# A decoder layer with a two-expert feed-forward part: places a half step later, gates' weights in steps, one sequence of expert tiles, deeper result and place buffers

## The chip, the core and the metric

One core of a Trainium2 chip runs the whole program. Its engines are TensorE (PE, with weight loads shown apart as PEld), VectorE (DVE), ScalarE (ACT), GpSimd (POOL) and SyncE (SP), which issues most of the DMAs. Each engine takes its instructions in the order in which they were written. The metric is the device time of one execution in microseconds (us); the time before is 1168.72 us, the median of three runs.

## What is computed

The reference is one pre-norm decoder layer on x of 64 sequences x 128 tokens x 128 features, in float32:

```
x = x + self_attention(layernorm(x))            # 16 heads of 8
x = x + cross_attention(layernorm(x), ctx)      # 77 context tokens, mask
x = x + ffn(layernorm(x))

ffn:  proj = x @ Wp.T;  scores = l2norm(proj) @ l2norm(sim).T / temperature     # 8 experts
      the two highest scores, softmax over the two -> weights
      out = sum over the two experts of weight * (gelu(x @ W1[e] + b1[e]) @ W2[e] + b2[e])
```

## The kernel before

**Attention.** A unit is one sequence (block); four blocks make a group (GB = 4), so there are 16 groups of self-attention jobs and then 16 of cross-attention. One loop (line 863) runs over all 128 blocks, each in two **half steps**; eight half steps are one group. A half step writes, in this order: PE's scores (`score_tiles`, L707, and the mask's bias, L716), DVE's maxima (L726) and ACT's exponentials (L753); then one entry of `soon`; statistics; then, in every second half step, a norm from `bits` and the values (L768), in the others entries of `todo` (the next group's transposes, query, key and value products, the output product) and a norm from `bits`; then **at most one entry of `late`, in the list's order, if its due half step has come**; then one scatter from `sending`; then, in three of eight half steps, one DMA of weights or constants. Scores use three PSUM banks (`ps_s`), of which a half step takes two; small products share two banks (`ps_m`, tag mm).

**The prologue of the next group** (line 608) is four norms through `bits`, then its products through `todo`. With its fourth norm it writes two POOL instructions: `add_row` (L233) and, for cross-attention, the mask's bias (L624).

**Routing.** After a cross group's output is added, `route(g)` (line 300) puts seven steps into `late`, due LATER = (6, 7, 8, 10, 11, 12, 13) half steps on: `trans` (L240), `project(0)` and `project(1)` (products with the gates' weights, L325; ACT's squares, L331; after the second, POOL's chain from ssq, L335, to rnorm, L212), `largest(0)` and `largest(1)` (DVE; the first begins with L345, which reads rnorm), `count` (POOL sums `ahead`, L381) and `place` (PE multiplies `both`, L391, and `ahead`, L394; DVE makes the places). Then eight scatters (L428, POOL, indirect DMA), one per half step, write the group's normalised rows to their places in `part.x` in DRAM, sorted by expert. Since a group takes eight half steps, the steps of one group lie between those of the next.

**Two parts.** Groups 0 to 10 are part 0 and groups 11 to 15 part 1, each with its own `part.x` and `part.y` in DRAM. `table(part)` finds which 256 rows and which expert each tile has. Unused rows are filled by DMAs from SP: `spare` (L274, 7 per part, written one per slot after the expert weights) and `tail_zeros` (L480). Scatters and tail zeros of a part are declared free of dependences among themselves (`apart`), and fetches wait for all that is in `part.scatters`; the spares are in neither.

**Gates' weights.** `finish_weights` (L106 to L111) and `gate_weights` (L286 to L298) prepare the cross-attention's biases and the product of the projection with the normalised expert vectors. They run once, through `todo`.

**Experts.** `experts(part)` (line 949) goes over the part's tiles (51 and 27). For tile t it writes `turn(t+1)` (transposes, L974; copy, L976; places `at`, L978), `hidden(t)` (L989, then ACT, L996), `output(t-1)` (L1007, DVE's addition L1013, and two scatters by POOL, L1018, to `part.y`) and `fetch(t+3)` (SP loads 256 rows, L961; DVE copies the expert's weights, L968). Results `yr` have three buffers, places `at` four; each is free when its scatters have landed or been read. Part 0's tiles begin beside the last half steps of the attention; later tiles are each followed by one entry of what is left of the lists (`rest`) and one scatter. Then part 1's tiles run as a second sequence, each followed by one or two gathers of part 0's results (L1048, SP) and their weighted sums (`combine`, L1054, DVE). At the end come the 20 gathers of part 1. All groups' rows stay in SBUF (`xs`) and leave as they are finished (L1059).

Of the kernel before, what the change touches and what calls it, by code (L numbers as in the profile page):

```python
# [15 lines left out]
P = 128  # L16
# [9 lines left out]
LATER = (6, 7, 8, 10, 11, 12, 13)  # L26
NORM = 2
SPLIT = 11
# [3 lines left out]
def decoder_layer(  # L32
# [71 lines left out]
    def finish_weights():  # L104

        nc.vector.tensor_scalar(W["bq_s"], W["bq_s"], float(DH) ** -0.5, None, ALU.mult)  # L106
        t = work.tile([P, P], F32, tag="bvb", name="bvb", bufs=1)
        nc.vector.tensor_copy(t, W["bv_s"].to_broadcast([P, P]))
        pb = ps_m.tile([P, D], F32, tag="mm", name="pb")
        nc.tensor.matmul(pb, t, W["co_s"], start=True, stop=True)  # L110
        nc.vector.tensor_tensor(W["bo_s"], pb, W["bo_s"], ALU.add)  # L111
# [145 lines left out]
    class Part:  # L257
# [14 lines left out]
        def spare(self, n):  # L272
            at = E * self.step + n * TILE
            nc.sync.dma_start(  # L274
                self.x[at : at + TILE, :].rearrange("(p h) d -> p h d", p=P), zero
            )

# [3 lines left out]
    def gate_weights():  # L281
# [9 lines left out]
        nc.gpsimd.tensor_scalar(sq, W["sim_s"], rn, None, ALU.mult)  # L291
        pt = ps_m.tile([P, E], F32, tag="mm", name="pt")
        nc.tensor.transpose(pt, sq, ident[:E, :E])
        snT = work.tile([P, E], F32, tag="snT", name="snT", bufs=1)
        nc.vector.tensor_copy(snT, pt)
        pg = ps_m.tile([P, E], F32, tag="mm", name="pg")
        nc.tensor.matmul(pg, W["wp_s"], snT, start=True, stop=True)
        nc.vector.tensor_copy(wpg[:, D:], pg)  # L298

    def route(g):  # L300
# [62 lines left out]
        def count():  # L363
# [23 lines left out]
            )  # L387

# [132 lines left out]
    newest, sending, clearing, gathered = [None], [], [], []  # L521
# [14 lines left out]
    def attention(beside):  # L536
# [293 lines left out]
        late, soon, now, bits, pieces, coming = [], [], [0], [], [], []  # L830
# [30 lines left out]
        steps, todo = [], []  # L861

        for s in range(NB + LAG + 3):
# [11 lines left out]
            if s == 13 * GB:  # L875
                todo.append(finish_weights)
                todo.append(gate_weights)
# [4 lines left out]
            for half in range(2):  # L882
# [10 lines left out]
                if soon:  # L893
                    soon.pop(0)()
                if half == s % 2 and n < NGRP:
# [41 lines left out]
        def rest():  # L937

            for queue in (soon, todo, bits, late, pieces):
                if queue:  # L940
                    f = queue.pop(0)
                    (f[1] if queue is bits or queue is late else f)()
# [6 lines left out]
    def experts(part, ff, ps_h, ps_y):  # L949
        flat = we_s.rearrange("p e w -> p (e w)")  # L950
        N = part.tiles
        V = [dict() for _ in range(N)]

        def fetch(t):
            v = V[t]
            v["x"] = ff.tile([P, 2, DX], F32, tag="x", name="xr", bufs=4)
# [13 lines left out]
        def turn(t):  # L970
# [6 lines left out]
            v["at"] = ff.tile([P, 2], I32, tag="at", name="at", bufs=4)  # L977
# [24 lines left out]
        def output(t):  # L1002
            v = V[t]
            py = ps_y.tile([P, 2, D], F32, tag="y", name="py")
# [7 lines left out]
            y = ff.tile([P, 2, D], F32, tag="y", name="yr")  # L1012
# [162 lines left out]
```

## Time and profile before

| | |
|---|---|
| runs | 1168.72, 1167.09, 1172.84 us |
| the profiled execution | 1172.9 us, span of its instructions 1171.2 us |
| PE busy | 1071.0 us (91%) |
| DVE, ACT, POOL busy | 748.3 (64%), 612.6 (52%), 603.7 us (52%) |
| mean granted PE clock | 0.948 |
| self-attention, about | 24 to 400 us |
| cross-attention, about | 400 to 819 us |
| expert tiles, PE | 817 to 1145.3 us |
| last gathers, sums and stores | 1145 to 1171 us |

How to read it: the page cuts the span into 40 equal slices; each digit is an engine's busy share in tenths, and PEclk is the clock that PE was granted. A list of waits gives the waiting line, what ended the wait, the total, the number of times and the longest. A timeline gives start, length, engine, line, operation and tiles (out<-in), and in brackets the idle time before with what ended it; a wait for several things is put down to the last of them that the profile shows, which need not be the true one. The letter q marks an engine's queue (an issue, not work). A table of stages gives each engine's busy time, the number of its instructions and the granted clock.

### The profile page before, as it was taken

Reading aid. Unit: us, or ns where it says so; the run is one execution under the profiler, and the core shown is the slowest. Engines: PE = TensorE matmul, PEld = TensorE weight load, DVE = VectorE, ACT = ScalarE, POOL = GpSimd, SP = SyncE. Lnnn points to the kernel's source line nnn. Section 1 sums busy time; section 2 is a strip of 40 time slices with the busy share of each in tenths; the row PEclk is TensorE's granted clock in tenths of the full one; section 3 lists DMA queues with packets and bytes.
Section 4 is the critical chain, followed back from the end, with each engine's and each line's share of the span. In section 5 each row is a group of like instructions: output and inputs, shape, how many; then the busy total and the mean of one; then the engine's idle time right before and its main releaser. Section 6 shows DMA issues by size and latency. Waiting matters only on the chain.

```text
span 1171.2 us, 39936 instructions
## 1 busy us (share of the span) xinstructions
PE 1071.0 (91%) x15925; PEld 874.9 (75%) x15925; DVE 748.3 (64%) x2139; ACT 612.6 (52%) x1378; POOL 603.7 (52%) x1313
## 2 busy tenths in 40 slices
PE   5999999999899999998889899999989899979990
PEld 3777777777677777776666677777888899969990
DVE  3588778788767656665656666776545454446655
ACT  3266556566556556664555556655545444424440
POOL 8122232232321323666565667667788886646661
PEclk9699999899989999998999989999989899989996
DMA  4233342333333322332222212221222242125544
GB/s 116 54 68 61 68 70 61 68 79 73 67 87 88 88 70 70 86 89 67 71 81 69 75 53 76 63 66 50 60 73 68 63 122 76 55 85 149 151 117 143
DMA packets 95561, 93.55 MB, mean 80 GB/s; under 512 B 23615, under 2 KB 77908, under 8 KB 95376
## 3 DMA queue, kind: packets, MB, share of 16 engines
q1 hardware_dynamic: 73280, 57.58, 22.1%
q0 software_dynamic: 9088, 16.94, 4.6%
q10 hardware_dynamic: 13008, 16.49, 4.5%
q8 instruction: 125, 2.05, 0.8%
q14 instruction: 60, 0.49, 0.2%
HBM read 49.69 MB, written 43.09 MB: 79 GB/s over the span
## 4 chain that ended last, share of the span: by engine, by line
PE 59%; DMA 13%; POOL 11%; issue 6%; DVE 6%; ACT 2%; SPq 2%; DVEq 0%; POOLq 0%; ACTq 0%
PE ps L707 12%; PE pt L707 9%; PE po L768 8%; PE py L1007 6%; PE ph L989 6%; POOL yr L1018 5%; DMA qh<-md 4%; PE pt L716 4%; PE ps L716 3%; DMA d<-kT 3%; PE pq L651 2%; POOL xr L428 2%; PE py L807 2%; PE pk L663 2%; PE tp L240 1%
## 5 line engine op out<-in xcount | busy, mean ns | idle before, releaser
L726 DVE TENSOR_REDUCE m<-ps 128x4 f32<-128x512 f32 (+1 forms) x512 | 275.0, 577 | 185.8 <-PE ps L716 105.4
L753 ACT ACTIVATE e<-pt 128x512 f32<-128x512 f32 (+1 forms) x512 | 277.0, 590 | 220.8 <-PE pt L716 113.8
L707 PE MATMUL pt<-qh,kh 32*128 32x128 f32 (+1 forms) x4096 | 325.2, 286 | 12.6 <-DMA qh<-md 10.8
L707 PE MATMUL ps<-kh,qh 31*128 31x128 f32 (+1 forms) x4096 | 327.6, 293 | 6.7 <-DVE m L726 4.7
L707 PEld LDWEIGHTS ps<-kh,qh 31*128 31x128 f32 x4096 | 276.6, 195 | 73.5 <-issue 31.7
L707 PEld LDWEIGHTS pt<-qh,kh 32*128 32x128 f32 (+1 forms) x4096 | 265.3, 169 | 18.8 <-issue 8.4
L996 ACT ACTIVATE hT<-ph,wr 128x256 f32<-128x256 f32 x312 | 128.6, 471 | 161.0 <-issue 127.7
L1018 POOL DMA_INDIRECT yr<-yr,at x156 | 165.9, 1064 | 87.0 <-DVE yr L1013 63.6
L428 POOL DMA_INDIRECT xr<-x,slot x128 | 133.2, 1041 | 73.8 <-ACT e L753 34.0
L217 POOL TENSOR_SCALAR var<-stat 128x4 f32<-128x4 f32 x48 | 11.1, 231 | 291.2 <-DVE stat L203 290.9
L1007 PEld LDWEIGHTS py<-wr,hT 128*128 128x128 f32 x1248 | 153.8, 194 | 8.9 <-DVE yr L1013 3.4
L1007 PE MATMUL py<-wr,hT 128*128 128x128 f32 x1248 | 154.6, 278 | 4.2 <-DVE yr L1013 4.2
L989 PE MATMUL ph<-xT,wr 128*128 128x256 f32 x624 | 152.1, 388 | 2.3 <-DVE at L978 1.8
L768 PE MATMUL po<-e,vm 128*32 128x128 f32 (+1 forms) x4096 | 145.2, 285 | 0.0
L768 PEld LDWEIGHTS po<-e,vm 128*32 128x32 f32 (+1 forms) x4096 | 108.8, 113 | 31.8 <-issue 24.3
L989 PEld LDWEIGHTS ph<-xT,wr 128*128 128x128 f32 x624 | 115.4, 195 | 16.3 <-issue 2.4
L716 PE MATMUL pt<-ident_b,bias 128*77 128x512 bf16 x256 | 96.0, 393 | 0.0
L1013 DVE TENSOR_TENSOR yr<-py,wr 128x256 f32<-128x256 f32 x78 | 33.1, 424 | 90.4 <-PE py L1007 90.1
L968 DVE COPY wr<-we_s 128x1157 f32 x78 | 61.6, 789 | 35.1 <-DVE yr L1013 32.5
L716 PE MATMUL ps<-bias,ident_b 128*128 128x308 bf16 x256 | 78.1, 310 | 0.0
L227 ACT ACTIVATE xn<-xs,shift,rstd 128x128 f32<-128x128 f32 x128 | 62.1, 491 | 28.0 <-POOL shift L221 8.1
L202 DVE BATCH_NORM_STATS2 st<-xs 128x6 f32<-128x128 f32 x192 | 54.4, 283 | 6.3 <-DMA xs<-in_x_dram 4.1
(173 smaller groups left out, 1351.4 us busy)
## 6 DMA issues: line engine op xcount, KB each, us to landing
xr<-xr SPq DMA_DIRECT2D x78, 130.0 KB
d<-qT ACTq DMA_DIRECT2D x32, 256.0 KB
qh<-d SPq DMA_DIRECT2D x128, 64.0 KB
r<-yr SPq DMA_DIRECT2D x64, 128.0 KB
d<-kT ACTq DMA_DIRECT2D x16, 256.0 KB
kh<-d SPq DMA_DIRECT2D x64, 64.0 KB
out_dram<-xs SPq DMA_DIRECT2D x16, 256.0 KB
xr<-zero SPq DMA_DIRECT2D x30, 130.0 KB
```

What stands on the lines that cost most here:

```text
L227: nc.scalar.activation(v["xn"][:, b, 0:D], xs[g][:, b, :], AF.Identity, bias=shift[:, i : i + 1], scale=rstd[:, i : i + 1],)
L428: i = nc.gpsimd.indirect_dma_start(out=part.x, out_offset=bass.IndirectOffsetOnAxis(ap=slot[:, g * GB + b, k : k + 1], axis=0), in_=v["xn" ...
L707: nc.tensor.matmul(pt[:, r, :], v[still][rows, r, b, :], v[moving][rows, r, b, :], start="bias" not in v or r == 0, stop="bias" not in v,)
L716: nc.tensor.matmul(pt, left, right.unsqueeze(1).to_broadcast([P, HG, K]), start=False, stop=True,)
L726: nc.vector.tensor_reduce(v["m", b // 2][:, c, :, b % 2], v.pop(("ps", b, c)), AX.X, ALU.max, negate=True,)
L753: i = nc.scalar.activation(e[:K], pt[:K], AF.Exp)
L768: nc.tensor.matmul(v["o"][32 * c : 32 * c + 32, b % 2, :, j // 2, :], w[:, at : at + 32], v["e", b, c][:K, j, :].rearrange("p (n q) -> p n ...
L968: nc.vector.tensor_copy(v["w"], flat[:, bass.ds(w, WE)])
L989: nc.tensor.matmul(ph[:, c % 2, :], v["w"][:, c * P : (c + 1) * P], v["xT"], start=True, stop=True,)
L996: i = nc.scalar.activation(v["h"][:, n, :], ph[:, n % 2, :], AF.Gelu, bias=v["w"][:, WF + n : WF + n + 1],)
L1007: nc.tensor.matmul(py[:, h, :], v["h"][:, c, h * P : (h + 1) * P], v["w"][:, F + c * D : F + (c + 1) * D], start=(c == 0), stop=(c == NFC ...
L1018: i = nc.gpsimd.indirect_dma_start(out=part.y, out_offset=bass.IndirectOffsetOnAxis(ap=v["at"][:, h : h + 1], axis=0), in_=y[:, h, :], in_ ...
```

## The change

- LATER's last entry goes from 13 to 14 (`place`), and after `count` the list `rest` skips two tiles.
- `finish_weights` and `gate_weights` become generators, of which one piece is written per half step, from block 52 on, instead of all in one half step.
- The spare rows' DMAs join the group `apart` and the list `part.scatters`.
- `experts` runs once over the tiles of both parts (78). `rest` and the scatters go on until 48 tiles have been output; the gathers of part 0 start once the first tile of part 1 has been output.
- Results `yr` have six buffers instead of three, places `at` eight instead of four.

```diff
--- before.py
+++ after.py
@@ -23,8 +23,9 @@
 NEG = -(2.0 ** 100)
 LAG = 4
 TILE = 256
-LATER = (6, 7, 8, 10, 11, 12, 13)
+LATER = (6, 7, 8, 10, 11, 12, 14)
 NORM = 2
+AHEAD = 3
 SPLIT = 11
 
 
@@ -106,8 +107,10 @@
         nc.vector.tensor_scalar(W["bq_s"], W["bq_s"], float(DH) ** -0.5, None, ALU.mult)
         t = work.tile([P, P], F32, tag="bvb", name="bvb", bufs=1)
         nc.vector.tensor_copy(t, W["bv_s"].to_broadcast([P, P]))
+        yield
         pb = ps_m.tile([P, D], F32, tag="mm", name="pb")
         nc.tensor.matmul(pb, t, W["co_s"], start=True, stop=True)
+        yield
         nc.vector.tensor_tensor(W["bo_s"], pb, W["bo_s"], ALU.add)
 
 
@@ -271,9 +274,11 @@
 
         def spare(self, n):
             at = E * self.step + n * TILE
-            nc.sync.dma_start(
+            i = nc.sync.dma_start(
                 self.x[at : at + TILE, :].rearrange("(p h) d -> p h d", p=P), zero
             )
+            apart(i.ins, f"x{self.n}")
+            self.scatters.append(i.ins)
 
     parts = [Part(0, 0, SPLIT), Part(1, SPLIT, NGRP)]
 
@@ -289,12 +294,17 @@
         nc.vector.reciprocal(sn, W["tmp_s"])
         nc.gpsimd.tensor_tensor(rn, rn, sn, ALU.mult)
         nc.gpsimd.tensor_scalar(sq, W["sim_s"], rn, None, ALU.mult)
+        yield
+        yield
         pt = ps_m.tile([P, E], F32, tag="mm", name="pt")
         nc.tensor.transpose(pt, sq, ident[:E, :E])
         snT = work.tile([P, E], F32, tag="snT", name="snT", bufs=1)
+        yield
         nc.vector.tensor_copy(snT, pt)
+        yield
         pg = ps_m.tile([P, E], F32, tag="mm", name="pg")
         nc.tensor.matmul(pg, W["wp_s"], snT, start=True, stop=True)
+        yield
         nc.vector.tensor_copy(wpg[:, D:], pg)
 
     def route(g):
@@ -385,6 +395,7 @@
             nc.gpsimd.tensor_tensor(
                 part.seen, ahead[:, GB - 1, :], both[:, GB - 1, :], ALU.add
             )
+            return "apart"
 
         def place():
             pr = ps_m.tile([P, GB * E], F32, tag="mm", name="pr")
@@ -518,7 +529,7 @@
             needs, sums, tails, experts_past, expert, tiles_past, first, places,
         ]
 
-    newest, sending, clearing, gathered = [None], [], [], []
+    newest, sending, clearing, gathered, ready = [None], [], [], [], [0]
 
     def apart(inst, group):
 
@@ -827,7 +838,7 @@
 
             soon.append(other)
 
-        late, soon, now, bits, pieces, coming = [], [], [0], [], [], []
+        late, soon, now, bits, pieces, coming, idle = [], [], [0], [], [], [], []
 
         def prepare(n):
 
@@ -858,7 +869,7 @@
         constants()
         clean(2)
         background = load_experts()
-        steps, todo = [], []
+        steps, todo, weights = [], [], []
 
         for s in range(NB + LAG + 3):
             if s == NB + 1:
@@ -873,8 +884,7 @@
                 if s // GB + 2 < len(jobs):
                     steps = prepare(s // GB + 2)
             if s == 13 * GB:
-                todo.append(finish_weights)
-                todo.append(gate_weights)
+                weights.extend((finish_weights(), gate_weights()))
             if s % GB == 3:
                 todo += steps
                 steps = []
@@ -892,6 +902,8 @@
                 arrived = len(coming)
                 if soon:
                     soon.pop(0)()
+                if weights and next(weights[0], weights) is weights:
+                    weights.pop(0)
                 if half == s % 2 and n < NGRP:
                     stats(s + 12)
                     if b == GB - 1:
@@ -936,23 +948,29 @@
 
         def rest():
 
+            if idle:
+                idle.pop()
+                return True
             for queue in (soon, todo, bits, late, pieces):
                 if queue:
                     f = queue.pop(0)
-                    (f[1] if queue is bits or queue is late else f)()
+                    if (f[1] if queue is bits or queue is late else f)() == "apart":
+                        idle.extend((None, None))
                     return True
             return False
 
         return rest
 
 
-    def experts(part, ff, ps_h, ps_y):
+    def experts(ff, ps_h, ps_y):
         flat = we_s.rearrange("p e w -> p (e w)")
-        N = part.tiles
+        order = [(part, t) for part in parts for t in range(part.tiles)]
+        N = len(order)
         V = [dict() for _ in range(N)]
 
         def fetch(t):
             v = V[t]
+            part, t = order[t]
             v["x"] = ff.tile([P, 2, DX], F32, tag="x", name="xr", bufs=4)
             v["w"] = ff.tile([P, WE], F32, tag="w", name="wr", bufs=4)
             row = nc.sync.value_load(
@@ -974,7 +992,7 @@
                 nc.tensor.transpose(tp[:, h * P : (h + 1) * P], v["x"][:, h, 0:D], ident)
             v["xT"] = ff.tile([P, TILE], F32, tag="xT", name="xT")
             nc.vector.tensor_copy(v["xT"], tp)
-            v["at"] = ff.tile([P, 2], I32, tag="at", name="at", bufs=4)
+            v["at"] = ff.tile([P, 2], I32, tag="at", name="at", bufs=8)
             nc.vector.scalar_tensor_tensor(
                 v["at"], v["x"][:, :, D], v["w"][:, WE - 1 :], v["x"][:, :, D + 1],
                 ALU.is_lt, ALU.add,
@@ -1001,6 +1019,7 @@
 
         def output(t):
             v = V[t]
+            part, _ = order[t]
             py = ps_y.tile([P, 2, D], F32, tag="y", name="py")
             for h in range(2):
                 for c in range(NFC):
@@ -1009,7 +1028,7 @@
                         v["w"][:, F + c * D : F + (c + 1) * D],
                         start=(c == 0), stop=(c == NFC - 1),
                     )
-            y = ff.tile([P, 2, D], F32, tag="y", name="yr")
+            y = ff.tile([P, 2, D], F32, tag="y", name="yr", bufs=6)
             nc.vector.tensor_tensor(
                 y, py, v["w"][:, WB : WB + D].unsqueeze(1).to_broadcast([P, 2, D]), ALU.add
             )
@@ -1024,7 +1043,6 @@
                 apart(i.ins, f"y{part.n}")
             v.clear()
 
-        AHEAD = 3
         for t in range(min(AHEAD, N)):
             fetch(t)
             yield
@@ -1037,6 +1055,7 @@
                 hidden(t)
             if t > 0:
                 output(t - 1)
+                ready[0] = t
             if t + AHEAD < N:
                 fetch(t + AHEAD)
             yield
@@ -1084,25 +1103,27 @@
                     pools.append(ctx.enter_context(tc.tile_pool(
                         name=name, bufs=bufs, space=bass.MemoryType.PSUM, reuse_waits="tile"
                     )))
-                first.append(experts(parts[0], *pools))
+                first.append(experts(*pools))
             if n < 4 or n > 4:
                 next(first[0])
 
         rest = attention(beside)
-        for _ in first[0]:
-            rest()
-            if sending:
-                sending.pop(0)([newest[0]])
-            if clearing:
-                clearing.pop(0)()
-        assert not rest() and not sending and not clearing
         ff = pools[0]
-
 
         done = [(g, b) for g in range(SPLIT) for b in range(GB)]
         total, steps = len(done), parts[1].tiles
-        for t, _ in enumerate(experts(parts[1], *pools)):
-            for _ in range(len(done) - total + min(total, (t + 1) * total // steps)):
+        for _ in first[0]:
+            t = ready[0] - parts[0].tiles
+            if t <= -AHEAD:
+                rest()
+                if sending:
+                    sending.pop(0)([newest[0]])
+                if clearing:
+                    clearing.pop(0)()
+            if t == -AHEAD:
+
+                assert not rest() and not sending and not clearing
+            for _ in range(len(done) - total + max(0, min(total, t * total // steps))):
                 if len(gathered) > 3:
                     combine()
                 gather(parts[0], ff, *done.pop(0))
```

## The prediction

> **What bounds the kernel now.** I read the slices of the page first, then what TensorE (PE) waited for, then the timelines around each wait.
>
> ```profile
> PE   5999999999899999998889899999989899979990
> PEclk9699999899989999998999989999989899989996
> ```
>
> PE is busy in nearly every slice, so time can only be won where it stands still or where its clock drops, and both digits dip in the same slices. The list of PE's waits names the places:
>
> ```profile
> PE pr L394 <- POOL ahead L381: 19.4, 9, 3.8
> ...
> PE tp L974 <- DMA xr<-xr: 8.6, 3, 7.8
> ...
> PE py L1007 <- DVE yr L1013: 4.2, 3, 3.0
> PE pt L293 <- POOL bvb L291: 3.5, 1, 3.5
> PE pb L110 <- DVE bvb L108: 2.3, 1, 2.3
> ```
>
> (total us, times, longest.) A wait costs more than its length. After the one at 545 us and the one at 318 us the stage table shows a granted clock (column PEclk) of 0.50:
>
> ```profile
> 318.70:328.90 10.20, 6.45 (x87) 5.34 (x90) 2.42 (x7) 1.87 (x5) 3.82 (x11) 0.50 0.37 89
> 547.40:554.20 6.80, 6.80 (x75) 4.82 (x74) 1.92 (x6) 2.67 (x5) 3.20 (x11) 0.50 0.32 62
> ...
> 239.00:246.00 7.00, 5.62 (x121) 4.14 (x124) 5.21 (x16) 3.73 (x8) 2.50 (x8) 1.00 0.23 41
> ```
>
> The third row follows an idle of 1.38 us (before 240.68) and keeps 1.00; an idle of 1.70 us (before 153.33) was followed by a half clock. So I price each wait by the length of its stage, not by the wait. The stages: in PE's timeline the first L707 product of every half step gives its start; eight half steps are one group.
>
> **Part A: spare rows out of the dependence chain.** Groups of the cross phase that start at 456.57, 481.67 and 507.45 last 25.10, 25.79 and 25.79 us. The next five (533.24 to 691.34) last 31.95, 30.19, 30.72, 31.69 and 33.55: 158.10 against 5 x 25.79 = 128.95, **29.15 us** too much. In just these the 14 spare-row DMAs (L274) are issued, 540.6 to 666.5:
>
> ```profile
> 540.63 0.36 SPq L274 DMA_DIRECT2D xr<-zero  x1
> ...
> 543.41 0.96 POOL L428 DMA_INDIRECT xr<-x,slot  x1 [4.05 <-ACT qT L654]
> 544.66 0.76 POOL L381 TENSOR_TENSOR ahead<-ahead,both 128x8 f32<-128x8 f32 x3
> ...
> 545.48 0.41 PE L394 MATMUL pr<-ahead,ones_f 128*128 128x32 f32 x2 [2.87 <-POOL ahead L381]
> ```
>
> ACT is named but was long done; the scatter starts 2.8 us after the spare DMA into the same tensor, about the 2.3 to 5.0 us a scatter takes to land. POOL waits for it, `ahead` is queued behind, and PE behind that. The diff puts the spares into the scatters' group, so neither waits for the other; fetches wait for them instead, over 130 us later, when they have long landed; SP issues the same 14 DMAs in the same places. Even if some wait stayed, the longest of these five PE waits (3.2) is about the half step (3.1 to 3.5) by which place moves. Gain 29.15; two shorter waits at 776.8 and 800.4 (0.61, 0.46) go too: **30.2**.
>
> The Trainium skill, "TensorE: Matmul & The Clock Gate", section "What's actually happening", says the clock halves after an idle window of about 3.4 us; by that none of these five waits (2.6 to 3.2 us) would halve it and A would give the 14.3 us of waits alone. The rows above disagree, so the sum goes by stage length.
>
> **Part B: place at 14 collides with trans.** A new group enters `late` every 8 half steps, its trans due at 6: the same half step as the previous group's 14. The eight scatters follow their place, one per half step, and still fill just eight. But the list pops one entry per half step, in order, so trans, project 0 and project 1 each slip one half step; largest 0 (due at 10) does not. The half step now free for project 1 is the one in which the next group's fourth norm issues add_row and bias on POOL, ahead of it. Today, in that half step (starts 501.85, the next 504.58):
>
> ```profile
> 506.65 0.20 POOL L212 TENSOR_TENSOR rnorm<-rnorm,newton 128x4 f32<-128x4 f32 x1
> ...
> 507.12 0.15 DVE L345 TENSOR_TENSOR gate<-raw,rnorm 128x32 f32<-128x32 f32 x1
> ...
> 507.52 2.00 DVE L357 TENSOR_TENSOR h<-gate,v 128x32 f32<-128x32 f32 x1
> ...
> 508.19 1.27 POOL L233 TENSOR_TENSOR xs<-xs,bo_s 128x512 f32<-128x512 f32 x1
> ```
>
> rnorm is ready at 506.85 and DVE needs it at 507.12: 0.27 us to spare. Afterwards POOL does, from the end of the fourth norm (505.66): L233 1.27, L624 1.27, small gaps, to 508.4, then the chain from ssq to rnorm, 2.70 (504.15 to 506.85): ready at 511.1. DVE is there at 507.12 + 0.66 (project's four matmuls, now in this half step) = 507.8 and **waits 3.3 us**; queued behind it are the maxima that free the score banks, and PE waits for those. In return L357 loses its 2.00 us: where no L233 runs beside it (769 us on) it takes 0.19. So largest 0 ends at 511.15 + 1.32 (its length at 815.41) = 512.5 instead of 510.5 (end of L361), 2.0 later; PE is itself 0.66 later there, having got that time back earlier in the group, so about **1.5 us** of new idle per group (the 0.2 us that PE waited there in 11 groups counted). 1.5 lies between the idles that kept (1.38) and lost (1.70) the clock; the group with the latter was 2.74 longer than its neighbours (22.94 against 20.20). I take 2.0. Bounds: -0.3 (the wait hidden, place's nine DVE instructions moved to an emptier half step) and 4.5 (3.3 in full, plus 1.2 of half clock). It happens in the 10 groups that still have a prologue to come: **+20**, bounds -3 and +45. The last three routed groups have no add_row but also lose their spare half step: +1.
>
> The Trainium skill, "SBUF — State Buffer", section "Who interferes with whom", says a DVE instruction with two SBUF inputs and a GpSimd one that reads SBUF block each other for the whole instruction; the 2.00 against 0.19 us agrees, and only this makes the new wait cheaper than its 3.3 us.
>
> **Part C: gates' weights in steps.** PE stands 316.39 to 323.99 except for five small products, at half clock to 328.9. The half steps there take 8.79, 3.89 and 2.65 against 2.47, 2.11 and 2.42 in the group before: 8.3 us. Spread over nine half steps, PE work remains (about 0.7). DVE's reciprocal (L289) still waits for ACT's square and half of POOL's chain, 319.49 to 321.39, with the next maxima queued behind it: 1.9, of which a half step absorbs some 0.5. I count 2 left (0 to 3): **-6.3**. The weights were issued by 238.4, so reading them from 301 on is safe.
>
> **Part D: deeper result and place buffers.** One line shows the present limit:
>
> ```profile
> 854.87 0.22 DVE L978 SCALAR_TENSOR_TENSOR at<-xr,wr 128x2 int32<-128x2 f32 x1 [6.09 <-issue]
> ```
>
> The place tile four back was still in use by a scatter, as POOL did two root chains (843.5 to 849.6). PE's hidden layers start at 850.60, 859.48 and 864.16 instead of 3.73 apart: 13.56 - 7.46 = **-6.1**. With eight, POOL may lag four tiles more (15 us). But the wait at 905.73 (1.85) comes from DVE waiting 2.37 for rnorm in the drained queue, at an unchanged distance from its project: it stays, and with POOL further behind I add **+1**.
>
> **Part E: two idle tiles after count.** The last place waited 3.75 (to 917.11): starts 909.54, 918.22, 924.26, i.e. 14.72 - 7.46 - 0.7 for its own products = 6.5. Two tiles are 7.5 us of cover: **-6.5**. Part 1's table then ends with tile 36 of the 51; its first fetch follows tile 48, so the delay is covered.
>
> **Part F: one sequence of tiles.**
>
> ```profile
> 1035.72 0.33 SPq L1048 DMA_DIRECT2D r<-yr  x1
> 1036.93 0.34 SPq L961 DMA_DIRECT2D xr<-xr  x1
> ...
> 1039.11 0.69 PE L974 MATMUL tp<-ident,xr 128*128 128x128 f32 x2 [7.76 <-DMA xr<-xr]
> ```
>
> On SP part 1's second fetch stands behind the first gather, which waits for the last result of part 0. The hidden layers at 1024.81 and 1046.72 are three tiles apart: 21.91 - 11.19 = 10.7. Afterwards five fetches precede the first gather. It still blocks SP for about two tiles, and the fetch behind it has about three. The gathers shift by five tiles to the end, where DVE has room (about 3.0 of 3.73 us per tile); the final 20 gathers wait for the last result as now. **-10.5**.
>
> **Sum.** -30.2 + 20 + 1 - 6.3 - 6.1 + 1 - 6.5 - 10.5 = -37.6. The profiled execution took 1172.9 us (span 1171.2 and 1.7 around it), near the slowest of the three runs; it goes to 1135.3, and the median of 1168.72 to **1131**.
>
> **Rivals.** (1) *The collision is hidden*: DVE catches up in the half steps that place leaves. For it: PE now waits only 4.7 us in 14 times for maxima. Against it: in that stretch DVE has no gap from 505.98 to the next group's third half step. Then +20 becomes 0: 1111. (2) *The wait at the seam only moves*: POOL lags by its deeper buffers, the first gather lands late, and the fetch behind it stalls PE for the 7.8 us seen now: 1139. For it: POOL busy 35.1 of 50 us in 950 to 1000; against it: no scatters remain to be sent there. (3) *Slower*: each collision costs what the worst of today's place waits cost, in the group at 657.79 (33.55 against 25.79, a wait of 2.92 and 10.2 us of half clock): 10 x 7.8 = 78 against gains of 57.6, i.e. 1189. It decides from 5.8 us per group. Against it: the wait is half as long. (4) *The change does not do what it says*: the spares still wait. Place's half step then covers the 3 us by itself, so the forecast stands.
>
> **Chances.** Forecast, with B between 1 and 4 us a group (1121 to 1151): 0.55. Rival 1 (1108 to 1121): 0.28. Rival 2 (1129 to 1150): 0.11. Rival 3: 0.03. Otherwise: 0.03. The range 1108 to 1152 leaves out some 0.1. Under 0.5% (6 us) cannot be told from no change here; the likely cases are all faster by more: 0.95 faster, 0.02 the same, 0.03 slower.
>
> **What would show it.** A and E right: PE's waits for `ahead` gone, groups beside the spares as long as their neighbours. B right: DVE's gate (L345) waits some 3 us for POOL in ten groups, L357 falls to 0.19 there, PE waits for maxima in the next half step but one, and the groups from 481 us on take 27 to 28 us. Wrong if L345 does not wait. C: no idle over 2 us near 310. F: no idle at the seam. The total is wrong above all if the half clock follows each new wait.

## The result and the profile after

The changed kernel takes **1202.66 us** (1200.19 to 1203.69) against 1167.9 us of the kernel before beside it: a ratio of **1.029 [1.025, 1.033]**. It is slower; forecast was 1131 us. The profiled execution took 1202.96 us, its span 1201.2 us, 30.0 more than before. Seven of the runs below (e7 to e13) were made beside a kernel before of 1170 to 1172 us and are compared in us; beside the other ten it took 1229 to 1233 us itself, with some half steps of every cross-attention group 1 to 2 us longer for no reason that the trace names (in e3 5.12 us for the 3.69 of the same kernel in e13), so those are read by their ratios among themselves and by the length of single waits.

The slices of the page, PE's busy share and its granted clock:

```profile
PE   5999999899999998998888889989999799999991
...
PEclk9799999999999999888888888889999999999996
```

Before, the clock dipped here and there; now it is down from slice 17 to 27 without a break. That is 480 to 811 us, the groups beside which routing runs. PE's waits (total us, times, longest) name one line above all, which was not on the short list of before (4.7 us in 14 times there), and a second one late in the expert part:

```profile
PE ps L718 <- DVE m L737: 47.6, 16, 4.5
...
PE ph L1007 <- DVE at L996: 7.6, 2, 6.8
```

What the change was to remove is gone from this list: no wait of place (`pr`) for `ahead`, none of the tile after the seam for its rows, none of the gates' weights. Instead PE waits for the maxima, ten times 4.46 or 4.47 us. The timelines of POOL, DVE and PE around the second of these (lines from the three engines' own timelines):

```profile
503.48 1.28 POOL L236 TENSOR_TENSOR xs<-xs,bo_s 128x512 f32<-128x512 f32 x1
507.43 1.27 POOL L635 TENSOR_SCALAR bias<-mask 128x308 bf16<-128x308 int32 x1 [2.68 <-PE pt L727]
508.79 0.24 POOL L345 TENSOR_SCALAR ssq<-ssq 128x4 f32<-128x4 f32 x1
...
511.07 0.20 POOL L215 TENSOR_TENSOR rnorm<-rnorm,newton 128x4 f32<-128x4 f32 x1
```

```profile
504.71 0.43 DVE L805 STREAM_TRANSPOSE aT<-t 128x256 f32<-128x256 f32 x1
511.31 0.19 DVE L355 TENSOR_TENSOR gate<-raw,rnorm 128x32 f32<-128x32 f32 x1 [6.16 <-POOL gap L438]
...
512.54 0.86 DVE L737 TENSOR_REDUCE m<-ps 128x4 f32<-128x308 f32 x2
```

```profile
506.96 0.38 PE L727 MATMUL pt<-ident_b,bias 128*77 128x512 bf16 x1
...
513.06 0.49 PE L718 MATMUL ps<-kh,qh 31*128 31x77 f32 x1 [4.47 <-DVE m L737]
```

Read them as one chain, backwards. PE's products at 513.06 wait for a score bank; the maxima that free it (512.54) stand on DVE behind `gate`, which waits 6.16 us for rnorm (since L805 ended at 505.14); rnorm stands on POOL behind `add_row` (L236) and `bias` (L635); and **bias itself has waited 2.68 us, for PE** (2.82 to 2.94 in the other nine groups): it needs a bias buffer that PE's products (506.96, ending 507.34) have just finished reading. So POOL waits for PE and PE, three steps on, for POOL. The stages behind such an idle (columns: busy us and number of PE, PEld, DVE, ACT, POOL; granted clock; DMA share; GB/s):

```profile
478.30:488.50 10.20, 10.11 (x103) 6.78 (x103) 6.24 (x24) 3.10 (x7) 4.36 (x12) 0.50 0.10 31
488.50:512.40 23.90, 20.09 (x356) 15.48 (x355) 10.15 (x36) 13.65 (x33) 13.30 (x31) 1.00 0.32 85
```

Each idle is followed by 10.2 us at half clock with PE busy all the time. A group lasts 34.13 to 34.68 us in ten groups; before, the five beside spare rows took 30 to 34 us and the others 25.5 to 25.9.

### The profile page after: what moved, and what is told of

Same layout as the page of the kernel before. It is cut to its first block, busy times and chain, and to the rows that moved or that the text cites. A ratio compares the mean times of both kernels' runs of the same rounds, so it can differ in the third digit from the quotient of the medians.

```text
span 1201.2 us, 39911 instructions
## 1 busy us (share of the span) xinstructions
PE 1089.9 (91%) x15925; PEld 884.5 (74%) x15925; DVE 730.0 (61%) x2139; ACT 611.1 (51%) x1378; POOL 601.5 (50%) x1313
## 4 chain that ended last, share of the span: by engine, by line
PE 76%; DMA 9%; POOL 5%; DVE 4%; ACT 3%; issue 2%; SPq 1%; DVEq 0%; ACTq 0%; POOLq 0%
PE ps L718 14%; PE py L1026 11%; PE ph L1007 11%; PE po L779 10%; PE pt L718 9%; PE pt L727 5%; PE ps L727 4%; DMA qh<-md 4%; PE pq L662 3%; DMA d<-kT 2%; PE py L818 2%; PE pk L674 2%; PE pv L688 2%; PE pp L335 1%; PE tp L992 1%
## 5 line engine op out<-in xcount | busy, mean ns | idle before, releaser
L718 PE MATMUL ps<-kh,qh 31*128 31x128 f32 (+1 forms) x4096 | 336.0, 297 | 47.9 <-DVE m L737 47.6
L718 PEld LDWEIGHTS ps<-kh,qh 31*128 31x128 f32 x4096 | 284.2, 199 | 124.0 <-DVE m L737 65.0
L718 PE MATMUL pt<-qh,kh 32*128 32x128 f32 (+1 forms) x4096 | 337.4, 292 | 11.2 <-DMA qh<-md 8.9
L718 PEld LDWEIGHTS pt<-qh,kh 32*128 32x128 f32 (+1 forms) x4096 | 275.0, 172 | 18.4 <-issue 9.0
L439 POOL DMA_INDIRECT xr<-x,slot x128 | 132.7, 1037 | 35.4 <-issue 17.5
L779 PE MATMUL po<-e,vm 128*32 128x128 f32 (+1 forms) x4096 | 148.6, 289 | 0.0
L779 PEld LDWEIGHTS po<-e,vm 128*32 128x32 f32 (+1 forms) x4096 | 110.9, 115 | 33.6 <-issue 25.1
L727 PE MATMUL pt<-ident_b,bias 128*77 128x512 bf16 x256 | 103.1, 418 | 0.0
L986 DVE COPY wr<-we_s 128x1157 f32 x78 | 61.7, 790 | 35.6 <-DVE yr L1032 33.0
L727 PE MATMUL ps<-bias,ident_b 128*128 128x308 bf16 x256 | 82.2, 326 | 0.0
L230 ACT ACTIVATE xn<-xs,shift,rstd 128x128 f32<-128x128 f32 x128 | 62.1, 491 | 30.2 <-POOL shift L224 9.7
L789 DVE STREAM_TRANSPOSE t<-po 128x512 f32<-128x512 f32 x64 | 44.9, 701 | 24.8 <-PE po L779 24.7
```

What stands on the lines that cost most here:

```text
L230: nc.scalar.activation(v["xn"][:, b, 0:D], xs[g][:, b, :], AF.Identity, bias=shift[:, i : i + 1], scale=rstd[:, i : i + 1],)
L439: i = nc.gpsimd.indirect_dma_start(out=part.x, out_offset=bass.IndirectOffsetOnAxis(ap=slot[:, g * GB + b, k : k + 1], axis=0), in_=v["xn" ...
L718: nc.tensor.matmul(pt[:, r, :], v[still][rows, r, b, :], v[moving][rows, r, b, :], start="bias" not in v or r == 0, stop="bias" not in v,)
L727: nc.tensor.matmul(pt, left, right.unsqueeze(1).to_broadcast([P, HG, K]), start=False, stop=True,)
L779: nc.tensor.matmul(v["o"][32 * c : 32 * c + 32, b % 2, :, j // 2, :], w[:, at : at + 32], v["e", b, c][:K, j, :].rearrange("p (n q) -> p n ...
L986: nc.vector.tensor_copy(v["w"], flat[:, bass.ds(w, WE)])
```

## The experiments

The questions: is it the order on POOL that costs; what are the parts of the 8.4 us per group; what do the other steps give without it.

**Kernels before and after once more, beside the next ones** (e0, no edit).

> The changed kernel once more, beside the kernels of this call. Theory (the loss is in the schedule, ten half clocks of 10.2 us after ten idles of 4.47 us): the same ten groups of 34.1 to 34.7 us, a ratio to the kernel before of 1.025 to 1.033 on a chip on which the latter takes about 1168 us. Rival (part of the difference belongs to the chip): another ratio, with the same ten groups in the changed kernel and longer groups in the kernel before.

> The kernel before once more, to see what its groups take on this chip. If chips do not differ: groups of 25.1 to 25.8 us apart from the five with spare rows (30 to 34 us), about 1168 us. If they do (1232 us was seen in the comparison runs of another chip): all ten groups above 28 us.

Measured: the changed kernel at 1.013 [1.010, 1.017] of the kernel before; eight of its groups again 34.1 to 34.4 us, the first 31.9 and the last 35.4; those of the kernel before take 29 to 34 us here. So eight of the changed kernel's ten groups are the same to 0.1 us in both surroundings; why is shown under e10. The rival holds: the smaller ratio comes from the kernel before, whose groups are longer.

**Place at 14 alone, in the kernel before** (e2).

```diff
-LATER = (6, 7, 8, 10, 11, 12, 13)
+LATER = (6, 7, 8, 10, 11, 12, 14)
```

> The kernel before with place's due half step at 14 and nothing else changed. Theory (the collision alone makes the loss): ten groups of about 34.2 us where the kernel before has 25.1 to 33.6 us (mean about 28.7), so 10 x 34.2 - 287 = +55 us, about 1224 us (1205 to 1245; above it if the spares' wait adds to the collision). Rival (the loss needs another part of the change beside it): the groups stay at 26 to 29 us and the time is within 1150 to 1175 us.

Measured: 1.020 [1.012, 1.027], groups of 34.1 to 35.6 us after a first of 31.8, DVE's waits for rnorm 67.6 us in 14, PE's ten idles 4.45 or 4.46 us. That is 24 us more and not the 55 expected, since the groups of the kernel before are longer here. The one number in LATER makes the idles; nothing else of the change is needed.

**Only project 1 late, place back at 13** (e6).

```diff
-LATER = (6, 7, 8, 10, 11, 12, 14)
+LATER = (6, 7, 9, 10, 11, 12, 13)
```

> The changed kernel with place back at 13, so that nothing collides, but project 1 due one half step later by itself (9 for 8). Theory (the order of project 1 against add_row and bias is enough): DVE waits about 6 us for rnorm in ten groups, PE idles 4 to 4.5 us in each, the groups take about 34 us and the time is that of the changed kernel, within 10 us. Rival (the crowding of place and trans in one half step is needed too): groups of at most 31 us, and a time at least 30 us below the changed kernel's.

Measured: 1.019 [1.011, 1.027], eleven groups of 33.4 to 36.9 us, each with an idle of PE of 4.45 to 4.47 us and a wait of DVE for rnorm of 5.8 to 6.1. Nothing collides here, and the loss is there: it is enough that project 1 comes behind `add_row` and `bias`.

**Two due entries in one half step, so that nothing slips** (e5).

```diff
                 if late and late[0][0] <= now[0]:
                     late.pop(0)[1]()
+                    if late and late[0][0] <= now[0]:
+                        late.pop(0)[1]()
```

> The changed kernel, place still due at 14, but two due entries of the list of routing steps may go in one half step, so that trans, project 0 and project 1 no longer slip. Theory (the slip of project 1 behind add_row and bias on POOL is what costs): DVE's wait for rnorm falls below 1 us and the ten groups fall from 34.2 us to those of the kernel with place at 13; about 80 us less than the changed kernel. Rival (place's nine DVE instructions in the half step of trans delay the maxima by themselves): the groups stay above 31 us and less than 30 us is gained.

Measured: 0.972 [0.964, 0.980], where the changed kernel had 1.013 beside the same kernel before: about 50 us less, between the 80 expected and the rival's 30; DVE's long waits for rnorm are gone. The groups were 28.4 to 31.6 there; e7 below, the same but for its buffers, shows nine of them at **25.57 to 25.86** and the last at 26.55. Place at 14 does no harm if nothing slips behind it.

**The slip kept, the two POOL instructions one half step later** (e9): `add_row` and `bias` move from the fourth norm to the start of the prologue's `trans`.

```diff
             def norm(b):
                 normalised(v, g, b)
-                if b < GB - 1:
-                    return
+
+            def trans():
                 add_row(g, W["bo_s"] if cross else bff_s)
...
-
-            def trans():
                 loads(n + 1)
```

> The changed kernel, place at 14 and the slip of project 1 kept, but add_row and bias issued one half step later, at the start of the prologue's trans, so that on POOL the chain from ssq to rnorm stands ahead of them again. Theory (the place of these two POOL instructions ahead of the chain is what costs): DVE's wait for rnorm falls from 6.2 to below 1.5 us, no idle of 4.5 us is left, and the time is that of the kernel in which two due entries may go in one half step, 0.97 to 0.98 of the kernel before. Rival (the slip itself, four products and a chain one half step later, is enough): idles of 2 us or more stay in ten groups, and the ratio is above 1.0.

Measured: 1125.51 us, 0.964 [0.956, 0.971]; groups of 25.88 to 25.94 us. POOL and DVE at the place of the fences above:

```profile
502.24 0.23 POOL L345 TENSOR_SCALAR ssq<-ssq 128x4 f32<-128x4 f32 x1 [0.50 <-ACT pp L341]
...
507.29 1.28 POOL L236 TENSOR_TENSOR xs<-xs,bo_s 128x512 f32<-128x512 f32 x1
508.66 1.27 POOL L635 TENSOR_SCALAR bias<-mask 128x308 bf16<-128x308 int32 x1
```

```profile
504.74 0.19 DVE L355 TENSOR_TENSOR gate<-raw,rnorm 128x32 f32<-128x32 f32 x1 [1.28 <-POOL gap L438]
```

Here the chain goes first, DVE waits 1.28 us and PE idles 0.36. Note the second thing: bias, now later, waits for nobody. The collision and the slip are as in the changed kernel, and with the queue's order the whole loss in the groups goes; how much of it was the order and how much the wait of bias, the next run tells.

**Four bias buffers for three** (e4, and again e11).

```diff
-                    v["bias"] = grp.tile([P, GB, S2], BF16, tag="bias", name="bias", bufs=3)
+                    v["bias"] = grp.tile([P, GB, S2], BF16, tag="bias", name="bias", bufs=4)
```

> The changed kernel with four bias buffers for three. Theory (a ring closes over the bias: POOL's bias waits 2.68 us for PE's products with an older one, and PE waits in turn for maxima queued behind the rnorm that follows that bias): POOL's wait for PE goes, DVE's wait for rnorm falls from 6.2 to about 3.5 us, PE's idle from 4.5 to about 1.8 us; with some half clock left the groups take 27 to 30 us, 1203 - 10 x (4 to 7) = 1130 to 1163 us. Rival (the queue order alone makes the loss, POOL's wait only fills time in which it would have waited anyway): groups of 33 to 34 us, 1190 to 1203 us.

> The changed kernel with four bias buffers for three. Theory (2.68 us of DVE's 6.16 us of waiting are the bias's own wait for PE): DVE waits 3.3 to 3.5 us as the prediction had it, PE idles about 1.8 to 2.2 us, the groups take 27.5 to 30.6 us depending on how long the clock stays halved; 40 to 65 us less than the changed kernel. Rival (the bias would have been late anyway): groups of 33 to 34 us.

Measured (e11): 1143.88 us, 0.979 [0.974, 0.985]; groups of 27.23 to 27.29 us after a first of 28.7. (e4: 0.976, groups of 28.8 to 30.6 us after a first of 32.3.) From e11's timelines and its list of PE's waits:

```profile
505.73 1.28 POOL L236 TENSOR_TENSOR xs<-xs,bo_s 128x512 f32<-128x512 f32 x1
507.10 1.27 POOL L635 TENSOR_SCALAR bias<-mask 128x308 bf16<-128x308 int32 x1
```

```profile
510.97 0.19 DVE L355 TENSOR_TENSOR gate<-raw,rnorm 128x32 f32<-128x32 f32 x1 [3.43 <-POOL gap L438]
```

```profile
PE ps L718 <- DVE m L737: 19.9, 16, 1.7
```

bias follows `add_row` at once, DVE waits 3.43 us and PE idles 1.73. These are the prediction's own numbers (3.3 and 1.5). So the prediction described a kernel with four bias buffers; the changed one has three. Of the 8.4 us, the wait of bias for PE makes 34.15 - 27.24 = **6.9**: 4.47 - 1.73 = 2.74 of idle, and the rest clock, for at 1.73 us the clock held in nine groups of ten.

**PE kept busy in the idle** (e10, e14): useless products ahead of the one that waits, into a bank that is overwritten next; 16 of them in e10, 8 in e14. The loop, without the lines that choose the half step:

```diff
...
+                    for _ in range(16):
+                        nc.tensor.matmul(
+                            ps, W["co_s"],
+                            W["co_s"][:, : ps.shape[-1]].unsqueeze(1).to_broadcast(
+                                [P, HG, ps.shape[-1]]
+                            ),
+                            start=True, stop=True,
+                        )
             for r in range(HG):
```

> The changed kernel with 16 products of 128x308 added ahead of the first score product of the ten half steps in which PE idles 4.47 us; they write a score bank that the next products overwrite, so nothing that is computed changes. Theory (of the 8.4 us by which a group grows, about half is the half clock that follows the idle): PE is busy with the added products (16 x 0.26 = 4.2 us), the clock stays at 1.00, and the groups take 25.8 + 4.2 = about 30 us, 10 x 4.2 = 42 us less than the changed kernel. Rival (the clock costs nothing there, since other engines set the pace after the idle): groups of 33 to 34 us.

> The changed kernel with 8 added products of 128x308 (two passes of 0.26 us each, 4.2 us together) ahead of the score product that waits; nothing that is computed changes. Theory (half of the loss is the half clock): the clock stays at 1.00 from 480 to 780 us, the groups take 25.05 + 4.2 to 4.5 = 29.3 to 29.8 us, and the time is 42 to 48 us below the changed kernel's, about 1157 us, though the wait for the maxima is as late as it was. Rival (the clock costs nothing there): 33 to 34 us a group, 1195 us or more.

Measured (e10): 1206.22 us, groups of 33.37. The products came one group early: the first of the ten groups that have them (at 449.6 us) has no idle without them (it takes 25.11 us in the changed kernel), and the last that idles (at 783.2) goes without. The added products took 16 x 2 x 0.26 = 8.3 us, not 4.2, since the trace shows each as two records (32 for 16 products); the expectation missed that, not the mechanism. The clock, and a stretch of added products in place of an idle:

```profile
PEclk8699999899999999999999999989999999999995
```

```profile
485.50:493.90 8.40, 8.40 (x35) 5.93 (x33) 3.79 (x17) 1.12 (x3) 6.33 (x14) 1.00 0.19 50
```

It is 1.00 throughout 347 to 790 us. The last group, in the same execution, idles 4.47 us, has 10.2 us at half clock and takes 34.55: longer than the groups that do 8.3 us of useless work. Without the added products a group takes 33.37 - 8.3 = 25.1 us. So of the changed kernel's 34.15, 4.47 are idle and, by subtraction, 34.15 - 25.1 - 4.47 = **4.6 are half clock**; e11 gives nearly the same another way (27.24 - 1.73 = 25.51; 34.15 - 25.51 - 4.47 = 4.2).

The changed kernel's own trace gives it a third way. After its idles 10.11, 9.57, 9.29 and then down to 9.03 us of half clock are left; PE is busy in them; if half of that is lost, it is 5.06 to 4.51 us. With this, nine of the ten groups are 25.15 + 4.47 + this half, to 0.02 us (34.68 = 25.15 + 4.47 + 5.06; 34.13 = 25.15 + 4.47 + 4.51). This also tells why eight groups had the same lengths in e0: the half clocks begin and end on a grid of 3.413 us (see the last section), a group that reaches its idle later on the grid has less half clock left, and so the groups settle at ten steps of it, 34.13 us.

With eight such products (e14) the clock held again from 325 to 768 us and the ratio fell to 0.988 [0.981, 0.995], against the 1.013 of e0: a kernel that does more, to no use, is some 2.5% faster. Its groups took 31.4 to 31.7 us in their middle, and the last, which has the idle and no added products, 35.3. They are above the 29.3 to 29.8 expected: beside a kernel before of 1233 us this says nothing on the split.

**Place at 13 with all the rest of the change** (e1, and again e12).

```diff
-LATER = (6, 7, 8, 10, 11, 12, 14)
+LATER = (6, 7, 8, 10, 11, 12, 13)
```

> The changed kernel with place's due half step back at 13, everything else as changed. Theory (the collision of place and trans is the whole loss): the ten groups of 34.2 us fall to the undisturbed 25.8 us, 10 x 8.4 = 84 us less, so 1203 - 84 = about 1118 us (1112 to 1126). Rival (another part of the change slows these groups, such as the spares in the scatters' group): the groups stay at 34 us and the time above 1190 us. If the spares still need place's cover: five groups of about 31 us come back, about 1148 us.

> The changed kernel with place's due half step back at 13. Theory: on a chip where undisturbed groups of the kernel before take 25.8 us, all ten groups take 25.5 to 25.9 us, 84 us less than the changed kernel, about 1117 us. Rival (the spares still delay POOL when place is at 13): five groups of 28 us or more, about 1130 to 1145 us.

Measured (e12): **1115.67 us**, 0.954 [0.949, 0.960]; all ten groups 25.49 to 25.91. (e1: 0.976, groups of 28.9 to 32.1.) The clock after the first slices:

```profile
PEclk9599999999999999999999999999999999999996
```

It holds without a break from 161 to 1093 us. The theory's number was 1117. The change without its place step beats both kernels.

**Step A alone, in the kernel before** (e3, and again e13).

```diff
-            nc.sync.dma_start(
+            i = nc.sync.dma_start(
...
+            apart(i.ins, f"x{self.n}")
+            self.scatters.append(i.ins)
```

> The kernel before with the 14 spare-row transfers in the scatters' group and nothing else changed. Theory (step A of the prediction): the five groups of 30 to 34 us fall to 25.8 us, -29 to -30 us, about 1139 us; PE no longer waits for ahead. Rival (the spares' wait was covered only because place moved, or the wait comes from something else): the waits for ahead stay, and the time is above 1160 us.

> The kernel before with the 14 spare-row transfers in the scatters' group and nothing else changed. Theory (step A): the five groups beside spare rows fall from 30 to 34 us to 25.8 us, 29 to 30 us less than the kernel before, about 1139 us. Rival: the waits for ahead stay, and less than 10 us is gained.

Measured (e13): 1139.36 us, 0.976 [0.970, 0.982], 1171.7 x 0.0244 = 28.6 us less (21 to 36 by the interval); the five groups beside spare rows take 25.48 to 25.78. (e3: 0.989, groups of 29 to 31 us with and without spare rows.)

**The expert part: buffers back, idle tiles added** (e7, e8, e15). e7 and e8 are e5's kernel, e15 is e12's. In e7 the buffers go back; in e8 and e15 the last project 1 is followed by two idle tiles:

```diff
-            v["at"] = ff.tile([P, 2], I32, tag="at", name="at", bufs=8)
+            v["at"] = ff.tile([P, 2], I32, tag="at", name="at", bufs=4)
...
-            y = ff.tile([P, 2, D], F32, tag="y", name="yr", bufs=6)
+            y = ff.tile([P, 2, D], F32, tag="y", name="yr")
```

```diff
                 inverse_root(v["rn"], v["ssq"])
+                return "apart"
```

> The kernel in which two due entries may go in one half step, with result and place buffers back at 3 and 4: step D undone. Theory (deeper buffers remove one stall of about 6 us early in the expert part and let POOL fall further behind, which lengthens the later wait for rnorm): an idle or a stretched tile returns near the first root chains, the idle before the last group's largest 0 shrinks by 2 to 5 us; in sum 0 to 8 us slower. Rival (the buffers have nothing to do with the later wait): the later idle is unchanged and the time 6 to 10 us slower.

> The kernel in which two due entries may go in one half step, with two idle tiles after the last project 1 as after count. Theory (in the expert part DVE waits for rnorm because largest 0 comes one tile after project 1 while POOL is some tiles behind): the idle of 3.4 us near 943 us and the half clock after it go, 5 to 10 us less. Rival (POOL is behind by more than two tiles, or what follows waits in its place): within 4 us of the kernel without.

> The changed kernel with place at 13 and two idle tiles after the last project 1 as well as after count. Theory (DVE waits for rnorm in the expert part because largest 0 comes one tile after project 1 while POOL is tiles behind): the idle of 3.5 us near 870 us shrinks to below 2 us; 2 to 8 us less than without the idle tiles, 1108 to 1114 us, 0.948 to 0.953 of the kernel before. Rival (what follows waits in its place): no difference, 0.954.

Measured: e7 1125.56 us, 0.963 [0.959, 0.966]; e8 **1115.68 us**, 0.954 [0.950, 0.958]; e15 0.977 [0.972, 0.982], the same as e1's 0.976. In e7 the stall of before is back, a tile of 9.19 us for 3.73 at 819.7 (an idle of 3.82); in e8, and in e12, it is absent. The late wait of `hidden` behind rnorm is 0.66 us in e7, 3.46 in e12 and 6.81 in the changed kernel; in e8 and e15, with the idle tiles, DVE's late `gate` waits for nothing. (PE's longest late idles in e7 and e8, 2.33 and 1.82 us, are put down to ACT's `hT`, not to rnorm.) So deeper buffers take one stall away; that they make the other longer fits these numbers, and about half of the 6.81 comes with place at 14, but e7 and e12 differ in more than the buffers. The idle tiles do what they were for; that they are worth having is not settled: e8 with them equals e12 without, and e15 shows no gain.

## Why the prediction was wrong

**The step that failed is part B**, as the prediction put it: "Afterwards POOL does, from the end of the fourth norm (505.66): L233 1.27, L624 1.27, small gaps, to 508.4, then the chain from ssq to rnorm, 2.70". The mechanism was right to the line: trans, project 0 and project 1 slip, largest 0 does not, DVE's `gate` waits for POOL, the maxima are queued behind, PE waits for them, L357's 2.00 us fall to 0.19. Two terms of its sum were mis-sized, the wait of 3.3 us and the half clock, and one was put at nothing without a reason: what L624 itself waits for.

| term, per group | predicted | measured |
|---|---|---|
| L624 (now L635) waits for a buffer | 0 | 2.68 to 2.94 |
| DVE waits for rnorm | 3.3 | 6.16 (e11, without that wait: 3.43) |
| PE idle | 1.5 | 4.47 (e11: 1.73) |
| half clock that follows | 0.5 | 4.2 to 4.6, by the trace 4.5 |
| sum | 2.0, at most 4.5 | 8.4 |

(Idle and half clock add up to 8.7 to 9.1; 0.29 us of idle was there before as well in eight groups, and where the rest of the difference to 8.4 goes stays open.)

The first is the cause of the others. The two instructions were moved with their lengths alone. In the trace of before L624 starts at 509.55, right behind L233, and the PE products whose buffer it takes end at 509.39:

```profile
509.01 0.38 PE L716 MATMUL pt<-ident_b,bias 128*77 128x512 bf16 x1
```

```profile
509.55 1.27 POOL L624 TENSOR_SCALAR bias<-mask 128x308 bf16<-128x308 int32 x1
```

It did not wait, but only because the chain and a scatter stood ahead of it and let it arrive 0.16 us after the release. Take the chain away from ahead of it and it arrives 2.7 us too early, and waits for what it always needed. One line of before's list of POOL's waits told it. It comes from the first three cross groups: in two neither the chain nor a scatter stood ahead (2.47 and 2.46 us, at 411 and 434 us), in the third the chain without a scatter (1.41, at 459):

```profile
POOL bias L624 <- PE pt L716: 6.3, 3, 2.5
```

The upper bound of 4.5 us failed for the same reason: it was built from the wait of 3.3 us, which was not itself bounded. The half clock failed as a size: 1.2 us stood in the upper bound and 0.5 in the value, where an idle of 4.47 us costs 4.2 to 4.6 more. The prediction had named this danger itself ("The total is wrong above all if the half clock follows each new wait"). Rival 3 named the right outcome with nearly the right price, 7.8 us a group against 8.4, and was given 0.03 because "the wait is half as long"; that was the same wrong term. That its price comes so close is in part luck: it was taken from another wait, of 2.92 us, with the same 10.2 us of half clock.

**The other steps**, from the runs without B:

| step | predicted | measured | from |
|---|---|---|---|
| A | -30.2 | -28.6 [-21, -36] | e13, ratio |
| B | +21 | +86 | spans, changed kernel less e12: 1201.2 - 1114.8 |
| C | -6.3 | -7.1 | two groups from 298.5: 49.18 us, from 294.2 in the changed kernel: 42.07 |
| D, E, F together | -22.1 | -21.3 in e12, -15.7 in the changed kernel | first product of the hidden layers to PE's end: 328.2, 306.9, 312.5 |
| all but B | -58.6 | -53 [-47, -60] | e12, ratio |

A's groups, C's stage and F's seam (in the changed kernel no idle, tiles 3.73 us apart through 1015 to 1094) came out as worked out. D removed its stall; what it added was sized at +1 and is about 1.5 in e12 (3.46 against 1.9 in before and e13), but in the changed kernel the late wait grew to 6.81 us with 6.8 us of half clock behind it. There, POOL reached ssq only at 953.76, behind four result scatters and two row scatters that it issued after DVE had read the products (944.66). One line each from the timelines of POOL and DVE:

```profile
953.76 0.24 POOL L345 TENSOR_SCALAR ssq<-ssq 128x4 f32<-128x4 f32 x1
```

```profile
956.28 0.19 DVE L355 TENSOR_TENSOR gate<-raw,rnorm 128x32 f32<-128x32 f32 x1 [7.31 <-POOL gap L438]
```

In e12 three result scatters and one row scatter stand there instead of four and two, 5.76 us from DVE's read (863.13) to ssq (868.89) instead of 9.10; the difference of 3.34 us is that of the two waits (6.81 - 3.46).

Rival 1 (the collision hidden) and rival 2 (the wait at the seam only moves) did not happen; rival 4 neither. With B at the predicted +21, the measured rest would have given 1115.7 + 21, about 1137 us, within the range. What stays open: why POOL is those two scatters further behind with place at 14, and what makes the groups longer when the kernel before takes 1230 us.

## What to carry to other kernels

When an instruction gets ahead of another in a queue, do not move its length alone: look up what it itself waits for and when that comes, for the instructions that used to stand ahead of it may have been the ones that hid its wait. A wait that does not appear in a profile has a margin, and the margin (here 0.16 us) is read from the end of its releaser, not from the list of waits. Where two engines wait for each other round a ring of buffers, one more buffer at the cheapest place (here a bias tile) can cut the ring. And an idle of PE may have to be paid twice: here 4.47 us as idle and some 4.5 as clock.

## What was not expected of the hardware

The length of an idle alone does not decide on the clock. In e11 an idle of 1.62 us (482.30 to 483.93) was followed by 3.4 us of half clock, and nine idles of 1.73 or 1.74 us, each at the same place in its group, by none; in the kernel before one of 1.70 lost it and one of 1.85 did not. Idles of 4.47 us lost it ten times in ten, for 10.2 us each, one of 6.81 for 6.8 (and for 10.2 in e11).

Where the idle falls counts too. In each trace the half clocks begin on one grid of 3.413 us, and last whole steps of it, 3.4, 6.8 or 10.2 us above (in e11 484.1 and 893.7 are 120 steps apart; in the changed kernel 478.3 and 512.4 are ten). On e11's grid the idle of 1.62 lies whole in one step (480.7 to 484.1), while each of the nine is cut by a border, with at most 1.35 us in one step. This fits those ten, but it is no sharp limit: a step of e11 with 1.13 us of idle (from 108.6) was followed by half clock, and in the kernel before one with 1.85 (from 902.3) was not. The Trainium skill, "TensorE: Matmul & The Clock Gate", section "What's actually happening", asks for an idle window of about 3.4 us; the 4.47 agree with it, the 1.62 do not.

A float32 product of 128x308 keeps PE some 0.52 us: in e10 16 of them are 32 records and take 8.4 us, 0.26 for each record, and one record is easily read as one product.
